# Cross-attention with layer norm: the last eight tiles in one written order, some residuals as identity products, and the last block's values' product in two halves

## The chip, the cores and the metric

The kernel runs on one core of one Trainium2 chip. Its time is the device time of one execution, in microseconds (us). A core has TensorE (PE, matrix products into PSUM), VectorE (DVE), ScalarE (ACT), GpSimd (POOL) and SyncE (SP), each with its own in-order instruction stream; they meet through semaphores. Loads, stores and copies are DMAs. SP, ACT and POOL each issue them in their own order, and all run on the same 16 DMA engines. Each text below that gives a time in us without more gives it from the start of the profiled span.

## The reference

Queries `x` (4 x 2048 x 512) attend to 77 context rows per batch, with 16 heads of 32; then a projection, a residual and a layer norm. All is float32.

```python
qs = (q @ wq).reshape(Bq, Lq, H, HD).transpose(0, 2, 1, 3)
ks_ = (k @ wk).reshape(Bq, Lk, H, HD).transpose(0, 2, 1, 3)
vs = (v @ wv).reshape(Bq, Lk, H, HD).transpose(0, 2, 1, 3)
scores = jnp.einsum('bhqd,bhkd->bhqk', qs, ks_) / jnp.sqrt(jnp.float32(HD))
scores = jnp.where(mask[:, None, :, :], -jnp.inf, scores)
attn_w = jax.nn.softmax(scores, axis=-1)
attn = jnp.einsum('bhqk,bhkd->bhqd', attn_w, vs)
...
out = attn @ wo + q
mu = jnp.mean(out, axis=-1, keepdims=True)
var = jnp.mean((out - mu) ** 2, axis=-1, keepdims=True)
return (out - mu) / jnp.sqrt(var + EPS) * gamma + beta
```

Here `k` and `v` are both the context, and the mask is the same for all rows of a batch.

## The kernel before, in words

The 8192 rows are cut into 64 tiles of 128 rows; two tiles make a block (32 blocks, 0 to 31), four tiles a group of the query projection. Keys and values of all batches are made once at the start. A tile then goes through these steps; names are those of the code.

1. `q_visit`, `q_evac` (L134, L145): a quarter of a group's queries on TensorE (12 products, each factor split into a high and a low float32r part), copied out by VectorE. They run five tiles ahead, so the last is issued in the slot of tile 58.
2. `scores` (L245): 16 products, one per head, into four PSUM banks. `maxima` (L262): VectorE adds the mask, writes the negated scores and keeps their minimum, one instruction per head. `exps` (L279): ACT's exponential, one per head, with the sum.
3. `recip` (L291) on VectorE and `normalise` (L295) on POOL divide by the sums; the last tile does it in two halves (`recip_half`, `normalise_half`).
4. `transp` (L314): VectorE transposes 32 x 32 squares of a tile into its half of the block's buffer `B`. `regroup` (L323): twelve SBUF-to-SBUF DMAs of 128 KB bring the squares of a block to the partitions of their keys, in `PT`.
5. `av` (L335): 16 products per block give the attention output, transposed. `av_hi` (ACT) and `av_lo` (VectorE) split it into two float32r parts, `AH` and `AL`.
6. `o_proj` (L370): 12 products per tile. `residual` (L385): VectorE adds the rows of `x`, loaded by `load_x` into one of eight buffers `o`. `moments` (L388): VectorE's statistics and aggregate, then POOL's power of -0.5, for two tiles at once.
7. `scale` (L412) on ACT and `affine` (L422) on POOL normalise; `store` (L427) on SP. For the last eight tiles `scale` is instead two VectorE instructions (subtract the mean and times gamma, times the root and plus beta), and there is no `affine`.

The order is written out by hand (`tc.manual_schedule()`): the order of the calls is the order of each engine's stream. A loop over pairs of tiles (L507) runs to the first half of slot 60; in slot u it does the scores of tile u, the projection of tile u - 6 or u - 5, and so on. L611 to L708 write out the rest. There block 30's twelve DMAs go to SP, SP and POOL in turn and block 31's to SP, ACT and POOL in turn; all others are SP's. One SP stream carries the x loads, the DMAs of `regroup` and the stores in the order of the calls; an x load must also wait until the tile eight before it is stored, since it takes its buffer. PSUM has eight banks, handed out in turn.

Of the kernel before, what the change touches and what calls it, by code (L numbers as in the profile page):

```python
# [36 lines left out]
TAILV = 8  # L37
LONE = 4
# [4 lines left out]
def xattn_layernorm(  # L43
# [39 lines left out]
    small = const.tile([P, 128], F32, name="small")  # L83
    mhalf, mneg, gates = small[:, 0:2], small[:, 2:4], small[:, 4:5]
# [218 lines left out]
    def recip_half(t, r):  # L303
        if r == 0:
            ris[t] = sb.tile([P, H], F32, tag="ri", bufs=3, name=f"ri_{t}")
        nc.vector.reciprocal(half_view(ris[t], r), half_view(sums[t], r))
# [7 lines left out]
    def transp(t):  # L314
        b, tt = divmod(t, 2)
        if tt == 0:
            bts[b] = sb.tile([P, 5, NP, 2, 32], F32, tag="B", name=f"B_{b}")
        nc.vector.transpose(  # L318
            bts[b][:, :, :, tt, :].rearrange("p c q r -> p q c r"),
# [3 lines left out]
    def regroup(b, queues=(nc.sync,)):  # L323
        pts[b] = sb.tile([P, 4, 2, NP * 2 * 32], F32, tag="PT", name=f"PT_{b}")
        pt = pts[b]
        bt = bts[b].rearrange("p c q t r -> p c (q t r)")
        n = 0
        for c in range(3):
            src = bt[:, 2:3].to_broadcast((P, 2, NP * 2 * 32)) if c == 2 else bt[:, c : c + 4 : 3]
            for i in range(4):  # L330
                queues[n % len(queues)].dma_start(pt[32 * c : 32 * c + 32, i], src[32 * i : 32 * i + 32])  # L331
                n += 1
# [17 lines left out]
    def av_hi(b, i):  # L350
        if i == 0:
            at[b] = [sb.tile([P, NG, BLK], F32R, tag=t, name=f"{t}_{b}") for t in ("AH", "AL")]
        nc.scalar.copy(at[b][0][:, 2 * i : 2 * i + 2], pas[b, i].rearrange("p (m r) -> p m r", m=2))

    def av_lo(b, i):
        hv = at[b][0][:, 2 * i : 2 * i + 2]
        pv = pas[b, i].rearrange("p (m r) -> p m r", m=2)
        nc.vector.tensor_tensor(at[b][1][:, 2 * i : 2 * i + 2], pv, hv.bitcast(F32), ALU.subtract)

    def av_evac(b):  # L360
        for i in range(2):
            av_hi(b, i)
            av_lo(b, i)
# [5 lines left out]

    def o_proj(t):  # L370
# [3 lines left out]
        pos[t] = bank(f"po_{t}")  # L374
        for c in range(NC_D):
            for n, (a, w) in enumerate(((ah, woh), (ah, wol), (al, woh))):
# [4 lines left out]
                    start=(c == 0 and n == 0),  # L381
# [6 lines left out]
    def moments(t):  # L388
# [9 lines left out]
        lone = t >= NT - LONE  # L398
        if lone or tt == 1:
            j = slice(tt, tt + 1) if lone else slice(0, 2)  # L400
            k = (t - tt) % TPB
            nc.gpsimd.tensor_tensor(rn[:, 0, j], mv[:, j, 1], nz[:, k + j.start : k + j.stop], ALU.add)
            nc.gpsimd.tensor_tensor(rn[:, 0, j], rn[:, 0, j], mhalf[:, j], ALU.pow)
            if t < NT - TAILV:
                nc.gpsimd.tensor_tensor(rn[:, 1, :], mv[:, :, 0], rn[:, 0, :], ALU.mult)
                nc.gpsimd.tensor_tensor(rn[:, 1, :], rn[:, 1, :], mneg, ALU.mult)

    def stats(t):
        residual(t)
        moments(t)  # L410

    def scale(t):  # L412
        o = od[t]
        b, tt = divmod(t, 2)
        mv, rn = mvs[b], rns[b]
        if t >= NT - TAILV:
            nc.vector.scalar_tensor_tensor(o, o, mv[:, tt, 0:1], gam, ALU.subtract, ALU.mult)  # L417
            nc.vector.scalar_tensor_tensor(o, o, rn[:, 0, tt : tt + 1], bet, ALU.mult, ALU.add)
        else:
            nc.scalar.activation(o, o, AF.Identity, bias=rn[:, 1, tt : tt + 1], scale=rn[:, 0, tt : tt + 1])  # L420
# [9 lines left out]

    nc.gpsimd.memset(mhalf, -0.5)
# [3 lines left out]
    warm = const.tile([P, D], BF16, name="warm")  # L435
    nc.vector.memset(warm, 0.0)
# [70 lines left out]
    for u in range(0, NT - 3, 2):  # L507
# [248 lines left out]
```

## Time and profile before

| what | value |
|---|---|
| runs shown | 547.81, 549.62, 550.54 us; median 549.62 |
| profiled execution, its own time | 546.65 us |
| its span | 544.7 us, mean granted TensorE clock 0.983 |
| busy share of the span | PE 96%, DVE 89%, ACT 85%, POOL 75% |
| scores of tile 56 start | 450.93 us |
| last projection (tile 63) ends | 530.5 us |
| last VectorE instruction ends | 541.55 us |
| store, from issue to landing, last stretch | 2.2 us (median) |
| x load, from issue to landing, last stretch | 3.6 us (median) |

In the lines of the trace, "line engine op, out<-in" names an instruction by its source line and the tiles it writes and reads; `po` is the projection's bank, `pa` the values' product, `sc` the scores, `nm` the row minimum. Busy times of PE come from a model of the pipelined ends of matmuls, so a busy PE is not one at its peak; what one matmul costs is read from one start to the next. SPq, DVEq and the like are an engine's sequencer, where a DMA issue or a wait stands. A wait is put down to the release that came last. The chain is the work that ended last, followed back from the end.

### The profile page before, as it was taken

How to read it: one execution, taken by the hardware profiler on the slowest of the kernel's cores; microseconds unless marked ns; L12 is line 12 of the kernel's file. 1: busy time of each engine (PE TensorE's matmuls, PEld its weight loads, DVE VectorE, ACT ScalarE, POOL GpSimd, SP SyncE). 2: the span in 40 equal slices, each digit the busy share in tenths (PEclk: the TensorE clock that was granted, in tenths of full speed). 3: DMA queues.
4: the chain of work that ended last, by engine and by line, in shares of the span. 5: the costliest groups of instructions: out<-in, count | busy, mean ns of one | idle time of the engine just before them, and what ended most of it. 6: DMA issues, size and time to landing. Idle time of an engine off the chain costs nothing.

```text
span 544.7 us, 15953 instructions
## 1 busy us (share of the span) xinstructions
PE 520.6 (96%) x4762; PEld 398.9 (73%) x4762; DVE 482.4 (89%) x2584; ACT 465.3 (85%) x2223; POOL 408.3 (75%) x354
## 2 busy tenths in 40 slices
PE   9999899999999999999999999999999999997790
PEld 6977577777777777777777777777777777775570
DVE  5687999989998889989998889989998889988677
ACT  5687799998899999998899999998899998889400
POOL 0526447888798988888798988888798986678651
PEclk9999999999999999999999999999999999998895
DMA  8935577778777877778778777778777766666752
GB/s 279 400 126 122 160 196 196 212 219 222 183 182 215 232 209 208 208 220 213 183 212 214 209 212 208 207 219 227 177 213 202 218 169 170 171 182 179 196 191 116
DMA packets 58982, 109.95 MB, mean 202 GB/s; under 512 B 9232, under 2 KB 10768, under 8 KB 58896
## 3 DMA queue, kind: packets, MB, share of 16 engines
q1 hardware_dynamic: 57088, 105.26, 69.8%
q0 software_dynamic: 1488, 3.15, 1.9%
q8 instruction: 38, 0.62, 0.5%
q10 hardware_dynamic: 320, 0.52, 0.3%
q14 instruction: 48, 0.39, 0.3%
HBM read 41.79 MB, written 16.78 MB: 108 GB/s over the span
## 4 chain that ended last, share of the span: by engine, by line
PE 79%; DVE 11%; SPq 4%; DMA 3%; issue 2%; ACT 1%; POOL 0%; DVEq 0%
PE po L377 29%; PE pq L131 27%; PE sc L254 11%; PE pa L342 10%; SPq L331 3%; DVE pbuf L268 3%; DVE B L318 2%; PE pk L157 1%; DMA stage_a<-wk 1%; DVE o L417 1%; DVE st L391 1%; DMA PT<-B 1%; DVE q L148 1%; DVE o L386 1%; ACT pbuf L282 1%
## 5 line engine op out<-in xcount | busy, mean ns | idle before, releaser
L282 ACT ACTIVATE pbuf<-pbuf,nm 128x77 f32<-128x77 f32 x1024 | 352.7, 352 | 34.6 <-DVE nm L268 33.1
L282 ACT ACTIVATION_READ_ACCUMULATOR pbuf<-pbuf,nm 128x1 f32 x1024 | 196.7, 192 | 0.0
L298 POOL TENSOR_TENSOR pbuf<-pbuf,ri 128x1232 f32<-128x1232 f32 x63 | 142.2, 2257 | 54.5 <-DVE ri L293 31.3
L268 DVE CUSTOM_DVE_ANT_0 pbuf<-sc,mb 128x77 f32<-128x77 f32 x1024 | 168.7, 231 | 5.4 <-PE sc L254 3.3
L377 PE MATMUL po<-woh,AH 128*128 128x512 f32 x256 | 107.4, 419 | 0.0
L318 DVE STREAM_TRANSPOSE B<-pbuf 128x1280 f32<-128x1280 f32 x64 | 95.6, 1493 | 7.4 <-DMA PT<-B 3.4
L377 PE MATMUL po<-wol,AH 128*128 128x512 f32 x256 | 101.1, 395 | 0.0
L377 PE MATMUL po<-woh,AL 128*128 128x512 f32 x256 | 100.6, 393 | 0.0
L131 PE MATMUL pq<-xth,wqh 128*128 128x512 f32 (+1 forms) x256 | 98.4, 384 | 1.3 <-DVE nm L268 1.3
L131 PE MATMUL pq<-xtl,wqh 128*128 128x512 f32 (+1 forms) x256 | 97.9, 382 | 0.0
L131 PE MATMUL pq<-xth,wql 128*128 128x512 f32 (+1 forms) x256 | 97.8, 382 | 0.0
L268 DVE DVE_READ_ACCUMULATOR2_ANT nm<- 128x1 f32 x1024 | 84.1, 82 | 0.0
L254 PEld LDWEIGHTS sc<-kct,q 32*128 32x128 f32 x2048 | 63.7, 186 | 22.5 <-issue 15.2
L425 POOL TENSOR_TENSOR o<-o,bet 128x512 f32<-128x512 f32 x56 | 73.3, 1310 | 4.4
L424 POOL TENSOR_TENSOR o<-o,gam 128x512 f32<-128x512 f32 x56 | 71.9, 1285 | 5.2 <-ACT o L420 5.2
L254 PE MATMUL sc<-kct,q 32*128 32x77 f32 x2048 | 73.4, 278 | 0.2 <-DVE nm L268 0.2
L342 PE MATMUL pa<-PT,vsb 96*32 96x256 f32 x1024 | 63.4, 388 | 6.9 <-DMA o<-x 3.8
L124 POOL TENSOR_TENSOR xtl<-xtf,xth 128x1024 fp32r<-128x1024 f32 x28 | 67.1, 2398 | 0.0
L377 PEld LDWEIGHTS po<-woh,AH 128*128 128x128 f32 x256 | 48.6, 190 | 24.3 <-DVE nm L268 9.0
L386 DVE TENSOR_TENSOR o<-po,o 128x512 f32<-128x512 f32 x64 | 43.9, 686 | 25.0 <-PE po L377 24.6
L131 PEld LDWEIGHTS pq<-xth,wqh 128*128 128x128 f32 x256 | 48.1, 188 | 11.8 <-DVE nm L268 2.3
L377 PEld LDWEIGHTS po<-woh,AL 128*128 128x128 f32 x256 | 48.5, 189 | 10.8
(87 smaller groups left out, 644.2 us busy)
## 6 DMA issues: line engine op xcount, KB each, us to landing
PT<-B SPq DMA_DIRECT2D x372, 128.0 KB, 2.4
o<-x SPq DMA_DIRECT2D x64, 256.0 KB, 5.2
out<-o SPq DMA_DIRECT2D x64, 256.0 KB, 2.7
xtf<-xT SPq DMA_DIRECT2D x28, 512.0 KB, 5.3
stage_a<-wq SPq DMA_DIRECT2D x4, 256.0 KB, 4.3
stage_a<-wk SPq DMA_DIRECT2D x4, 256.0 KB, 5.9
stage_b<-wv SPq DMA_DIRECT2D x4, 256.0 KB, 5.0
stage_a<-xT SPq DMA_DIRECT2D x2, 512.0 KB, 7.0
```

The source lines that it names most:

```text
L124: nc.gpsimd.tensor_tensor(l, fx.pop((g, c)), h.bitcast(F32), ALU.subtract)
L131: nc.tensor.matmul(pq, w[:, c, m * P : (m + 1) * P], r[:, c, rs], start=(n == 0), stop=(n == 11))
L254: nc.tensor.matmul(sc[j][:, g * NK : (g + 1) * NK], qs[q, g, rs], kct[q, g, t // TPB, keys_of(j)], start=True, stop=True,)
L268: nc.vector.tensor_tensor_reduce(pb[:, h // 2, (h % 2) * NK : (h % 2 + 1) * NK], scs[t][j][:, g * NK : (g + 1) * NK], mb[:, t % TPB, keys_ ...
L282: nc.scalar.activation(pb[:, h // 2, (h % 2) * NK : (h % 2 + 1) * NK], pb[:, h // 2, (h % 2) * NK : (h % 2 + 1) * NK], AF.Exp, bias=nmax[t ...
L298: nc.gpsimd.tensor_tensor(pv, pv, rv.to_broadcast((P, NP, 2, NK)), ALU.mult)
L318: nc.vector.transpose(bts[b][:, :, :, tt, :].rearrange("p c q r -> p q c r"), pbuf[t % NPB].rearrange("p q (c r) -> p q c r", c=5),)
L342: nc.tensor.matmul(pas[b, g // 2][HD * j : HD * (j + 1), (g % 2) * BLK : (g % 2 + 1) * BLK], vsb[:, 2 * b // TPB, HD * h : HD * (h + 1)], ...
L377: nc.tensor.matmul(pos[t], a[:, c, rs], w[:, c, :], start=(c == 0 and n == 0), stop=(c == NC_D - 1 and n == 2),)
L386: nc.vector.tensor_tensor(od[t], pos.pop(t), od[t], ALU.add)
L424: nc.gpsimd.tensor_tensor(o, o, gam, ALU.mult)
L425: nc.gpsimd.tensor_tensor(o, o, bet, ALU.add)
```

## The change

From slot 56 on, the loop and the written-out end are replaced by a string of 325 words, each one call of a helper, run in that order; so the streams of all engines are set by one list. A word is a letter and a tile (or block) number counted from tile 48 (block 24); T and e take a quarter of the heads, P and U one DMA of `regroup` with the queue that issues it (s is SP, a is ACT, g is POOL). Besides the order:

- Tiles 54, 55, 56, 57, 58, 60, 62 and 63 get their residual from TensorE: `resid` multiplies a 128 x 128 identity by the rows of `x` into the bank of the projection, which then accumulates on it. Statistics and centring of these tiles read PSUM.
- Fourteen tiles (50 to 63) end with `centre` and `finish` on VectorE, where eight did, and each has its own root on POOL (`rsqrt_one`).
- Block 31 is kept tile by tile in `B` and `PT`; `regroup_tile` issues twelve DMAs of half size for each tile, `av_tile` multiplies one tile, and the split into high and low parts goes by tile.
- The DMAs of blocks 27 to 31 are spread over SP and POOL, with ten on ACT.
- The identity is made once by POOL in slot 0, in the bytes of the tile that warms TensorE up.

```diff
@@ -34,8 +34,28 @@
 EPS = 1.0e-5
 WARM = 10
 NPB = 3
-TAILV = 8
-LONE = 4
+LAST = 16
+
+
+
+
+
+ORDER = """
+S8 Q8 q7 x4 T8.3 T8.0 e8.3 T8.1 T8.2 S9 k1 q8 x5 e8.1 f1 t7 S10 e8.2 T9.2 P3.7s O2 T9.0 k0 P3.1g x6 T9.1 e8.0
+P3.8s P3.10g T9.3 f0 P3.6s T10.2 Q9 e9.2 P3.9s T10.3 w1 +2 x7 e9.1 r8 T10.0 n8 w0 s2 P3.4s V2 e9.3 P3.11s T10.1
+q9 P3.5s e10.1 P3.3g y2 P3.0s S11 t8 v2 x8 a2.0 Q10 a2.1 P3.2g e9.0 b2.0 T11.3 T11.1 e11.3 r9 x9 T11.0 n9 O3
+b2.1 e10.0 q10 T11.2 e10.3 t9 S12 e10.2 z2 P4.5g P4.10s V3 T12.2 P4.4g w2 e11.1 r10 P4.8s P4.0g +3 n10 P4.2s
+T12.1 O5 e11.0 P4.7s s3 P4.1s e11.2 T12.0 P4.6s P4.3g y3 P4.9s t10 v3 S13 e12.2 P4.11s O4 a3.1 r11 T12.3 n11
+a3.0 T13.0 e12.1 b3.0 b3.1 e12.0 T13.1 S14 t11 e12.3 X6 z3 P5.5g O6 e13.1 T13.2 P5.10g w3 P5.0s T14.2 P5.4g
+e13.0 T13.3 P5.9g P5.3s r12 P5.2s T14.1 n12 V4 e13.2 P5.7s +4 P5.6s T14.0 e13.3 P5.8s s6 P5.11g S15 P5.1s T14.3
+a4.0 x10 y6 X7 a4.1 r13 e14.3 t12 n13 O7 e14.2 b4.0 T15.0 v6 e14.1 s4 V5 T15.1 v4 e14.0 b4.1 t13 X10 a5.1 e15.1
+X8 r14 P6.7g P6.1s y4 P6.9g X9 x11 T15.2 e15.0 P6.11s P6.4g z4 O8 P6.8g b5.1 w4 a5.0 P6.6g z6 e15.2 +5 n14 w6
+P6.2s T15.3 P6.10a O9 P6.3s h15.0 s5 P6.5a x12 m15.0 b5.0 P6.0s e15.3 s7 v5 t14 O10 y5 U14.9a U14.5g h15.1
+U14.10g y7 U14.3a U14.8g V6 z5 U14.0g U14.4a s8 w5 m15.1 U14.7s U14.6a s9 U14.11s X12 v8 t15 a6.0 O11 a6.1 v7
+x13 b6.0 U15.2a U15.7s b6.1 U15.4g U15.6s U14.2a y8 U15.5g U15.11s O12 z7 U15.0g U14.1a U15.8s y9 U15.10a x14
++11 v9 w7 s10 U15.1s U15.3g O13 z8 U15.9g y10 s11 v10 x15 s12 v11 W14 +13 v12 s13 W15 c14 y12 X14 c15 d14 v13
+d15 X15 z9 O14 y13 y11 z12 z10 w12 w8 O15 z11 z13 s14 w13 w11 y14 w10 w9 v14 s15 y15 v15 z14 z15 w14 w15
+"""
 KSCALE = 1.0 / HD**0.5
...
+    ident = const.tile([P, D // 2], F32, name="ident")
+    warm = ident.bitcast(BF16)
+    ident = ident[:, :P]
...
@@ -314,22 +337,32 @@
     def transp(t):
         b, tt = divmod(t, 2)
         if tt == 0:
-            bts[b] = sb.tile([P, 5, NP, 2, 32], F32, tag="B", name=f"B_{b}")
+            bts[b] = sb.tile([P, 5, 2 * NP * 32], F32, tag="B", name=f"B_{b}")
+        if b < NBLK - 1:
+            bt = bts[b].rearrange("p c (q t r) -> p c q t r", q=NP, t=2)[:, :, :, tt, :]
+        else:
+            bt = bts[b].rearrange("p c (t q r) -> p c q t r", q=NP, t=2)[:, :, :, tt, :]
         nc.vector.transpose(
-            bts[b][:, :, :, tt, :].rearrange("p c q r -> p q c r"),
+            bt.rearrange("p c q r -> p q c r"),
             pbuf[t % NPB].rearrange("p q (c r) -> p q c r", c=5),
         )
 
-    def regroup(b, queues=(nc.sync,)):
-        pts[b] = sb.tile([P, 4, 2, NP * 2 * 32], F32, tag="PT", name=f"PT_{b}")
-        pt = pts[b]
-        bt = bts[b].rearrange("p c q t r -> p c (q t r)")
-        n = 0
-        for c in range(3):
-            src = bt[:, 2:3].to_broadcast((P, 2, NP * 2 * 32)) if c == 2 else bt[:, c : c + 4 : 3]
-            for i in range(4):
-                queues[n % len(queues)].dma_start(pt[32 * c : 32 * c + 32, i], src[32 * i : 32 * i + 32])
-                n += 1
+    def regroup_part(b, n, queue, cols=slice(0, 2 * NP * 32)):
+
+        if b not in pts:
+            pts[b] = sb.tile([P, 4, 2, 2 * NP * 32], F32, tag="PT", name=f"PT_{b}")
+        c, i = divmod(n, 4)
+        bt = bts[b][32 * i : 32 * i + 32, :, cols]
+        src = bt[:, 2:3].to_broadcast((32, 2, cols.stop - cols.start)) if c == 2 else bt[:, c : c + 4 : 3]
+        queue.dma_start(pts[b][32 * c : 32 * c + 32, i, :, cols], src)
+
+    def regroup(b):
+        for n in range(12):
+            regroup_part(b, n, nc.sync)
+
+    def regroup_tile(t, n, queue):
+        tt = t % 2
+        regroup_part(t // 2, n, queue, slice(tt * NP * 32, (tt + 1) * NP * 32))
...
+    def av_tile(t):
+        b, tt = divmod(t, 2)
+        pt = pts[b].rearrange("p i a (t q r) -> p i a t q r", q=NP, t=2)
+        pas[b, tt] = bank(f"pa_{b}_{tt}")
+        for g in range(NG):
+            for j in range(GH):
+                h = g * GH + j
+                nc.tensor.matmul(
+                    pas[b, tt][HD * j : HD * (j + 1), g * P : (g + 1) * P],
+                    vsb[:, t // TPB, HD * h : HD * (h + 1)],
+                    pt[:NK2, :, h % 2, tt, h // 2],
+                    start=True,
+                    stop=True,
+                )
+
+    def at_part(b, k, i, by_tile):
+        if by_tile:
+            return at[b][k][:, :, i * P : (i + 1) * P], pas[b, i].rearrange("p (m r) -> p m r", m=NG)
+        return at[b][k][:, 2 * i : 2 * i + 2], pas[b, i].rearrange("p (m r) -> p m r", m=2)
...
+    def resid(t):
+        pos[t] = bank(f"po_{t}")
+        nc.tensor.matmul(pos[t], ident, od[t], start=True, stop=False)
 
     def o_proj(t):
         b, tt = divmod(t, 2)
         rs = slice(tt * P, tt * P + P)
         ah, al = at[b]
-        pos[t] = bank(f"po_{t}")
+        first = t not in pos
+        if first:
+            pos[t] = bank(f"po_{t}")
...
-                    start=(c == 0 and n == 0),
+                    start=(first and c == 0 and n == 0),
...
+    def moments_one(t):
+        st = sb.tile([P, 6], F32, tag="st", bufs=3, name=f"st_{t}")
+        nc.vector.bn_stats(st, pos.get(t, od[t]))
+        mvs[t, 1] = sb.tile([P, 4], F32, tag="mvt", bufs=LAST - 2, name=f"mvt_{t}")
+        nc.vector.bn_aggr(mvs[t, 1][:, :2], st)
+
+    def rsqrt_one(t):
+        mv = mvs[t, 1]
+        k = t % TPB
+        nc.gpsimd.tensor_tensor(mv[:, 2:3], mv[:, 1:2], bat[t // TPB][1][:, k : k + 1], ALU.add)
+        nc.gpsimd.tensor_tensor(mv[:, 2:3], mv[:, 2:3], mhalf[:, :1], ALU.pow)
+
+    def centre(t):
+        nc.vector.scalar_tensor_tensor(od[t], pos.pop(t, od[t]), mvs[t, 1][:, 0:1], gam, ALU.subtract, ALU.mult)
+
+    def finish(t):
+        nc.vector.scalar_tensor_tensor(od[t], od[t], mvs[t, 1][:, 2:3], bet, ALU.mult, ALU.add)
...
-    for u in range(0, NT - 3, 2):
+    for u in range(0, NT - LAST // 2, 2):
...
+            nc.gpsimd.memset(ident, 0.0)
+            nc.gpsimd.affine_select(ident, ident, [[-1, P]], ALU.not_equal, 1.0, base=0, channel_multiplier=1)
...
-    A, L = NT - 3, NBLK - 1
-    scores(A)
-    maxima(A, 0, H)
-    recip(A - 1)
-    normalise(A - 1)
-    affine(A - 8)
-    av(L - 3)
-    av_hi(L - 3, 0)
...
+    T0, B0 = NT - LAST, NBLK - LAST // 2
+    q4, by = H // 4, {"s": nc.sync, "a": nc.scalar, "g": nc.gpsimd}
+    one = {
+        "S": scores, "r": recip, "n": normalise, "t": transp, "W": av_tile, "x": load_x, "X": resid, "O": o_proj,
+        "+": residual, "s": moments_one, "v": rsqrt_one, "y": centre, "z": finish, "k": scale, "f": affine, "w": store,
+    }
+    for word in ORDER.split():
+        op, arg = word[0], word[1:]
+        k = None
+        if "." in arg:
+            arg, k = arg.split(".")
+        t, b = T0 + int(arg), B0 + int(arg)
+        if op in one:
+            one[op](t)
+        elif op in "Te":
+            (maxima if op == "T" else exps)(t, q4 * int(k), q4 * int(k) + q4)
+        elif op in "hm":
+            (recip_half if op == "h" else normalise_half)(t, int(k))
+        elif op in "Qq":
+            (q_visit if op == "Q" else q_evac)(*divmod(t + 5, 4))
+        elif op == "P":
+            regroup_part(b, int(k[:-1]), by[k[-1]])
+        elif op == "U":
+            regroup_tile(t, int(k[:-1]), by[k[-1]])
+        elif op == "V":
+            av(b)
+        elif op in "ab":
+            (av_hi if op == "a" else av_lo)(b, int(k))
+        else:
+            (av_hi if op == "c" else av_lo)(t // 2, t % 2, True)
```

## The prediction

> **What bounds the kernel now.** I read the page's slices first, to see which stages have slack. For 38 of 40 slices TensorE is full, so nothing outside it can matter there; the end is different.
>
> ```profile
> PE   9999899999999999999999999999999999997790
> DVE  5687999989998889989998889989998889988677
> ACT  5687799998899999998899999998899998889400
> POOL 0526447888798988888798988888798986678651
> ```
>
> Next the windows by stage, from the slot of tile 56 (its scores start at 450.93, by the timeline) to the end. Columns: window, its length, busy time of PE, weight loads, DVE, ACT and POOL, granted clock, DMA share, GB/s.
>
> ```profile
> 420.00:430.00 10.00, 10.00 (x123) 7.37 (x121) 9.77 (x65) 9.59 (x46) 8.45 (x9) 1.00 0.74 221
> 450.00:460.00 10.00, 10.00 (x117) 7.70 (x119) 9.77 (x57) 8.16 (x42) 6.59 (x8) 1.00 0.53 157
> 480.00:490.00 10.00, 9.81 (x98) 7.06 (x100) 9.90 (x68) 8.43 (x43) 6.82 (x8) 1.00 0.68 189
> 490.00:500.00 10.00, 7.23 (x99) 5.47 (x102) 8.50 (x47) 10.00 (x57) 8.30 (x7) 0.93 0.76 196
> 505.00:510.00 5.00, 2.00 (x9) 1.31 (x7) 2.93 (x6) 4.50 (x21) 2.89 (x3) 1.00 0.90 247
> 510.00:515.00 5.00, 4.18 (x37) 2.68 (x38) 3.40 (x4) 1.17 (x2) 2.50 (x5) 0.72 0.37 97
> 530.00:535.00 5.00, 0.49 (x3) 0.06 (x1) 4.69 (x9) 0.00 (x0) 1.16 (x2) 0.77 0.31 119
> 535.00:540.00 5.00, 0.00 (x0) 0.00 (x0) 4.72 (x9) 0.00 (x0) 1.15 (x2) 0.50 0.36 140
> ```
>
> The reader is to see two things. TensorE starves at 495 and 506 (and its clock falls with it), and it is done at 530.5, while VectorE then works alone for 11 us on a backlog that it could not start earlier. The chain of what ended last names both places, and VectorE's waits from 452 on say what it stood for:
>
> ```profile
> 495.18 2.40 DMA PT<-B
> 497.78 2.93 PE pa L342 x32
> 506.87 3.86 DMA o<-x
> 540.80 0.75 DVE o L418
> ```
>
> ```profile
> DVE AL L358 <- ACT AH L353: 4.2, 3, 3.0
> DVE o L386 <- PE po L377: 3.5, 3, 1.5
> DVE B L318 <- POOL pbuf L312: 2.0, 1, 2.0
> DVE ri L293 <- ACT pbuf L282: 1.3, 1, 1.3
> DVE ri L306 <- ACT pbuf L282: 0.4, 1, 0.4
> ```
>
> That is 11.4 us of standing. (The x load named at 506.87 rides behind the last PT pieces; the product needs the pieces.) So from 450.93 on the question is how densely VectorE's list can be packed, and whether TensorE's list is then still shorter.
>
> **Part by part: VectorE's list.** Before the new slots it ends the loop as it does now (first row maximum at 452.07). Start-to-start prices from the timeline: a row maximum 0.158 (16 took 2.53); a q copy, a low part (L358) 0.60; a reciprocal 0.17; a transpose 1.42; a residual add 0.70; statistics with aggregate 0.83; centre and finish together 1.47 (532.43 to 533.87 is 1.44, 538.44 to 539.95 is 1.51). Today: 128 maxima 20.2, 4 copies 2.4, 9 reciprocals 1.5, 9 transposes 12.8, 12 low parts 7.2, 14 adds 9.8, 14 statistics 11.6, 8 pairs 11.8, together 77.3. From 452.07 to the end of the last finish, 541.55, are 89.5, so 12.2 are idle, which agrees with the 11.4 of listed waits.
>
> The change takes 8 adds off (X on tiles 54 to 58, 60, 62, 63: -5.6) and brings 6 more pairs (tiles 50 to 55 get their scale and affine on VectorE: +8.8). The list grows to 80.5. So the change costs VectorE 3.2 and can win only out of the idle 12.2.
>
> How much idle stays? The densest stretches above (9.77, 9.77, 9.90 of 10) have 1.0 to 2.3% idle; with the list now offering at every point a finish, a centre or a quarter of maxima that needs nothing new, I take 2.3% of 80.5, 1.9, and one wait of the size that a residual had at 517 (0.5): 2.4. Bounds: 0.8 (the best stretch) and today's 12.2. I take the low side because the places of today's idle are covered by name: the low part's 4.2 and the transposes' 2.0 were chains with nothing else queued on VectorE, and the order now puts finishes (z3, z4, z6), centres and statistics of older tiles behind each.
>
> From the last finish to the end of the span is 544.7 - 541.55 = 3.15. New is that eight stores (2.1 MB) wait for the last eight microseconds, seven of them behind store 60 on SP's in-order queue. At 313 GB/s (517 to 519) they need 6.7, against about 7 that VectorE takes from that store's release to the last: 0.3 more.
>
> Sum: 452.07 + 80.5 + 2.4 + 3.15 + 0.3 = 538.4, against 544.7: 6.3 less.
>
> **TensorE's list**, which must stay shorter. Prices: scores 1.06, a q group 2.81, a values' product 1.86, an output projection 2.82. 8 scores 8.5, 3 groups 8.4, 5 products 9.3, the last block's two half products 1.9 (half the columns each), 14 projections 39.5, and 8 identity products. No full-array fp32 matmul is in the trace. The values' product moves 16 times 256 columns in 1.86 on a quarter of the columns of the array: 0.45 ns a column if nothing overlaps (512 columns: 0.23), 1.82 if four share the array (0.93). The scores move 16 times 77 in 1.06, which with four sharing is 3.4 ns (1.76). I take 0.93, from the longer rows, which are nearest in length; 7.4 in all, between 1.8 and 14.1. Sum 75.0, so 525.9 without a wait; behind the last projection follow statistics 0.83, two POOL steps 1.29 (0.605 and 0.684), a finish 0.75, hand-overs 0.25 and the store 3.45: 6.6, together 532.5. It may wait 5.9 before it decides. [...]
>
> **What is not on the path.** ACT from 452.4: 128 exponentials at 0.343 are 43.9, 12 casts 6.2, 2 scales 1.5 (6 scales fewer, -4.5), ten new DMA issues at 1.02 (4 took 4.08) 10.2: 61.8 of 80; the U issues stand behind the last exponentials, and only the casts of blocks 30 and 31 queue behind them. POOL: normalising 8 times 2.26 and 2 times 1.22, affines only for tiles 48 and 49 (5.3; six fewer, -16), 14 root pairs at 1.29, 27 DMA issues at 0.55 where 8 were: 59. A normalise can stand behind a root or a few issues, 1 to 2 us late, covered by the two tiles between it and its product. SP: 35 pieces, 12 loads and 16 stores at 0.60, 38. The identity's memset and select fall in POOL's 7.6 idle before 34.37; between 0.3 and 1.3 by its rows, hidden; were they not, the first normalise would be that much late. The last block's pieces go from 12 to 24 of half size, but over three queues; block 31's twelve took 8.3 from transpose to product today.
>
> [...] Eight statistics and eight centres now read PSUM instead of SBUF. By the rows, the add from PSUM (674 ns) costs no more than the statistics from SBUF (694) or the centre (732), and the copy from PSUM 669: no surcharge. [...]
>
> **Rivals.**
> - *The waits stay (slower).* TensorE is in order, and X15 stands ahead of the last two projections. Its load needs the buffer of tile 55, whose store stands behind finish 55 and ahead of the load on SP: 2.2 (median store in the last stretch) plus 3.6 (load) = 5.8 from store to data, against one projection, two half products and X14, 5.6, on TensorE. X14 and X12 hang in the same way. Each miss empties VectorE as 506 does now (3.86). If idle stays at 12.2, the span is 548.2, 3.5 more. It breaks even at 8.7 idle: two such misses. Against it: the buffers are eight deep and the other loads lie far ahead.
> - *TensorE becomes the bound.* At 1.76 an identity product the list is 81.7, to 532.6; with 4 of the 7.1 us of waits it has today after 495 (2.77, 3.82, 0.52), and 6.6 behind, 543.2, 1.5 less: no change to speak of.
> - *Denser still.* Idle 0.8 and stores unhindered: 536.5, 8.2 less.
>
> **How the numbers follow.** The profiled execution took 546.65 around its span of 544.7, and lies 3.0 under the median of 549.62 (547.81 to 550.54); I take the difference from the median. Forecast, 549.6 - 6.3 = 543.3, own range 541.8 to 546.0: 0.58. Denser, 541.4: 0.14. TensorE bound, 548.1: 0.14. Waits stay, 553.1: 0.14, some of it within half a per cent. Half a per cent is 2.75, about what a measurement of this kernel can tell from no change. Faster 0.58 + 0.14 + a little of the middle: 0.74; same 0.13; slower 0.13. The range takes the first three with the scatter of the median, 1: 540.3 to 549.0.
>
> **What would show it.** VectorE's waits after 452 sum to 3, not 11; no window of 5 us after 490 with VectorE under 4.4 before the last; TensorE's granted clock stays at 1.00 from 490 to 525; the last projection ends between 527 and 532; identity products near 0.93 start to start; centres near 0.73. Wrong would be: a wait of TensorE for an x load in front of L419, identity products over 1.5, or VectorE standing over 8.

## The result, and the profile after

The changed kernel takes 541.26 us (median of four, 540.0 to 543.51) against 548.71 (547.7 to 550.54) for the kernel before, measured together: a ratio of 0.9865, 95% interval 0.9817 to 0.9914. The profiled execution took 540.23 us around a span of 538.5, where the one before took 546.65 around 544.7. So it is 6.4 us less in the profiled pair and 7.5 in the medians; forecast were 6.3 less, a span of 538.4 and a median of 543.3.

First the page's slices of the kernel after, busy tenths of each fortieth of the span:

```profile
PE   8999899999999999999999999999999999999795
DVE  5688899889999898889998998889999988999977
```

VectorE and TensorE now go down together, in the last slice. Then the windows by stage, with the columns as shown of before, and the sums over all windows from 450 on:

```profile
490.00:500.00 10.00, 10.00 (x105) 5.98 (x97) 9.97 (x45) 8.91 (x46) 5.63 (x9) 1.00 0.41 105
505.00:510.00 5.00, 3.63 (x16) 2.66 (x15) 4.91 (x8) 0.78 (x5) 2.89 (x6) 1.00 0.91 261
510.00:515.00 5.00, 3.56 (x38) 2.20 (x39) 3.33 (x5) 1.17 (x2) 4.48 (x11) 1.00 0.76 236
520.00:525.00 5.00, 5.00 (x77) 3.82 (x76) 3.85 (x10) 0.97 (x2) 2.08 (x7) 1.00 0.20 56
525.00:530.00 5.00, 5.00 (x21) 3.62 (x20) 5.00 (x8) 0.20 (x1) 0.21 (x1) 1.00 0.06 24
530.00:535.00 5.00, 1.93 (x9) 1.27 (x7) 4.86 (x10) 0.00 (x0) 1.48 (x4) 0.91 0.76 290
...
sum 95.00, PE 76.53 PEld 55.62 DVE 79.70 ACT 53.14 POOL 53.37; mean PE 5.47 PEld 3.97 DVE 5.69 ACT 3.80 POOL 3.81
```

The starved window of before at 505 to 510 (TensorE 2.00, VectorE 2.93) has VectorE at 4.91 now, and the granted clock holds at 1.00 to 530. What is left of the hole lies at 508.6 to 511.4, on TensorE. VectorE's waits from 452 on (total, times, longest):

```profile
DVE o L439 <- PE po L430: 1.5, 2, 1.0
DVE AL L410 <- ACT AH L406: 1.1, 1, 1.1
DVE B L345 <- POOL mvt L483: 0.8, 1, 0.8
DVE st L475 <- PE po L430: 0.7, 1, 0.7
DVE B L345 <- POOL pbuf L335: 0.4, 1, 0.4
DVE pbuf L291 <- PE sc L277: 0.3, 1, 0.3
```

They sum to 4.8, where before had 11.4. TensorE's waits over the same time, 5.4 in all:

```profile
PE pa L375 <- DMA PT<-B: 2.8, 1, 2.8
PE po L430 <- DVE nm L291: 1.5, 2, 1.0
PE po L419 <- DVE nm L291: 1.1, 1, 1.1
```

And the chain of what ended last, in order of time (start, length):

```profile
508.80 2.66 DMA PT<-B
511.45 1.92 PE pa L375 x32
513.38 1.05 PE po L419 x2
514.43 8.22 PE po L430 x36
...
526.82 1.32 DVE o L486 x2
528.14 2.65 DVE o L489 x4
530.79 0.62 DVE st L475
```

It goes from the pieces through TensorE to the projection of tile 61, and then along VectorE to the end. TensorE's last product starts at 531.54, VectorE's last statistics at 532.32, the last finish ends at 535.34. Before, TensorE was done at 530.5, and VectorE worked on for 11 us more. (The chain's first line starts at 508.80, at an issue of POOL that by the order is a piece of tile 62; the wait is for block 30, whose last piece is SP's of 506.24, shown below.)

### The profile page after: what moved, and what is told of

Its sections match the earlier page's. It is cut to its first block, busy times and chain, and to the rows that moved or that the text cites. A ratio compares the mean times of both kernels' runs of the same rounds, so it can differ in the third digit from the quotient of the medians.

```text
span 538.5 us, 16101 instructions
## 1 busy us (share of the span) xinstructions
PE 522.8 (97%) x4810; PEld 398.9 (74%) x4810; DVE 483.6 (90%) x2588; ACT 462.6 (86%) x2217; POOL 404.5 (75%) x367
## 4 chain that ended last, share of the span: by engine, by line
PE 76%; DVE 13%; DMA 4%; SPq 2%; ACT 2%; issue 1%; POOL 1%; DVEq 0%; ACTq 0%
PE po L430 29%; PE pq L154 26%; PE sc L277 10%; PE pa L375 9%; DVE pbuf L291 4%; DVE B L345 3%; DMA PT<-B 3%; SPq L357 1%; ACT pbuf L305 1%; PE pk L180 1%; DMA stage_a<-wk 1%; DVE o L486 1%; DVE q L171 1%; DVE AL L410 1%; DVE o L489 1%
## 5 line engine op out<-in xcount | busy, mean ns | idle before, releaser
L305 ACT ACTIVATION_READ_ACCUMULATOR pbuf<-pbuf,nm 128x1 f32 x1024 | 216.4, 211 | 0.0
L291 DVE DVE_READ_ACCUMULATOR2_ANT nm<- 128x1 f32 x1024 | 84.7, 83 | 0.0
L277 PE MATMUL sc<-kct,q 32*128 32x77 f32 x2048 | 72.1, 277 | 0.0
L467 POOL TENSOR_TENSOR o<-o,bet 128x512 f32<-128x512 f32 x50 | 65.7, 1314 | 3.9
L466 POOL TENSOR_TENSOR o<-o,gam 128x512 f32<-128x512 f32 x50 | 64.3, 1286 | 0.2
L375 PE MATMUL pa<-PT,vsb 96*32 96x256 f32 x992 | 60.2, 382 | 3.0 <-DMA PT<-B 2.8
L439 DVE TENSOR_TENSOR o<-po,o 128x512 f32<-128x512 f32 x56 | 38.5, 687 | 22.4 <-PE po L430 22.2
```

Source lines behind the costliest of these rows:

```text
L277: nc.tensor.matmul(sc[j][:, g * NK : (g + 1) * NK], qs[q, g, rs], kct[q, g, t // TPB, keys_of(j)], start=True, stop=True,)
L291: nc.vector.tensor_tensor_reduce(pb[:, h // 2, (h % 2) * NK : (h % 2 + 1) * NK], scs[t][j][:, g * NK : (g + 1) * NK], mb[:, t % TPB, keys_ ...
L305: nc.scalar.activation(pb[:, h // 2, (h % 2) * NK : (h % 2 + 1) * NK], pb[:, h // 2, (h % 2) * NK : (h % 2 + 1) * NK], AF.Exp, bias=nmax[t ...
L375: nc.tensor.matmul(pas[b, g // 2][HD * j : HD * (j + 1), (g % 2) * BLK : (g % 2 + 1) * BLK], vsb[:, 2 * b // TPB, HD * h : HD * (h + 1)], ...
L439: nc.vector.tensor_tensor(od[t], pos.pop(t), od[t], ALU.add)
L466: nc.gpsimd.tensor_tensor(o, o, gam, ALU.mult)
```

## The experiments

To compare runs, the "stretch" is the span less the start of tile 56's scores (450.77 to 452.46 in all kernels): 93.8 us before, 87.2 after. The table has the profiled executions. VectorE's busy time is the sum of the windows from 450 to 545; "lost" is the time that TensorE's work in that stretch lost to a granted clock under 1.00 (busy time times what is missing from 1.00, by windows of 1 us).

| run | us | stretch | VectorE busy | VectorE waits | PE waits | lost |
|---|---|---|---|---|---|---|
| before | 546.65 | 93.8 | 78.0 | 11.4 | 6.8 | 3.4 |
| after | 540.23 | 87.2 | 79.7 | 4.8 | 5.4 | 0.0 |
| after_again | 543.01 | 90.4 | 79.2 | 8.3 | 5.7 | 3.1 |
| e1_no_ident | 545.17 | 92.5 | 84.7 | 4.7 | 10.8 | 3.9 |
| e9_before_ident | 549.99 | 96.3 | 77.0 | 16.0 | 7.6 | 6.5 |
| e2_whole_block | 543.4 | 90.4 | 80.0 | 7.8 | 5.4 | 3.3 |
| e3_one_queue | 546.23 | 93.0 | 82.0 | 8.8 | 8.2 | 3.4 |
| e4_ident_twice | 543.56 | 90.9 | 79.6 | 8.3 | 2.6 | 0.0 |
| e5_stats_twice | 548.84 | 94.6 | 86.3 | 6.8 | 7.5 | 2.6 |
| e7_four_act_pool | 548.58 | 95.3 | 75.1 | 17.8 | 7.8 | 6.2 |
| e6_piece_first | 539.64 | 86.6 | 79.8 | 4.2 | 4.8 | 0.0 |
| e8_both | 540.19 | 86.5 | 78.9 | 5.5 | 4.2 | 0.0 |
| e10_warm_after | 542.5 | 89.7 | 79.4 | 7.6 | 4.2 | 1.7 |
| e11_warm_before | 547.36 | 94.2 | 78.3 | 12.0 | 5.9 | 0.0 |

In nearly every row the stretch is VectorE's busy time plus its waits plus 2 to 3.5 (before has 4.4, e11 3.9, e5 1.5). That is bookkeeping, since VectorE works to the end in every kernel; it does not say what sets the end. The runs say what each part of the change does to these two terms. Those called e1 to e5, e7, e9 and after_again are single executions, run beside one of the kernel before (548.02 us for e1 to e4, 552.95 for the others), and the executions of the kernel before lie between 546.65 and 552.95.

**The same kernel again.** No edit.

> The changed kernel once more, to see how far the stretch from tile 56's scores to the end (87.2 in its profile) scatters between executions: every theory expects 87.2 within 0.5.

It took 543.01, 2.8 more than the profiled execution above, with the same list and 3.5 more of waits on VectorE. The stretch is 90.4, and not within 0.5 of 87.2 as expected. That is as much as several edits below move, so a single execution is read with the table, not by its time alone. The difference has a place. In windows of 1 us, this run of the unchanged kernel shows TensorE at half clock right behind the wait for block 30's pieces:

```profile
509.00:510.00 1.00, 0.00 (x0) 0.00 (x0) 0.62 (x2) 0.00 (x0) 1.00 (x2) 1.00 0.97 291
510.00:511.00 1.00, 0.00 (x0) 0.00 (x0) 0.95 (x1) 0.00 (x0) 0.88 (x4) 0.81 0.94 258
511.00:512.00 1.00, 0.79 (x8) 0.45 (x12) 0.56 (x1) 0.00 (x0) 0.69 (x2) 0.50 0.84 274
517.00:518.00 1.00, 1.00 (x5) 0.75 (x4) 1.00 (x2) 0.00 (x0) 0.00 (x0) 0.77 0.43 109
518.00:519.00 1.00, 1.00 (x6) 0.82 (x5) 0.20 (x1) 0.00 (x0) 0.00 (x0) 1.00 0.83 145
```

The wait was 3.1 here and 2.8 above, where the clock stayed up. The values' product then took 3.6 instead of 1.9, and the last product of TensorE started at 534.35 instead of 531.54.

**No identity products.** All X words dropped, the add of VectorE put back in front of the statistics:

```diff
-X6 ... X7 ... X10 ... X8 ... X9 ... X12 ... X14 ... X15
+(none)
-s6    s7    s8    s9    s10    s12    s14    s15
+ +6 s6 +7 s7 +8 s8 +9 s9 +10 s10 +12 s12 +14 s14 +15 s15
```

> The changed kernel without identity products: the eight residuals go back to VectorE as adds, each ahead of its tile's statistics; the order is otherwise the same. All runs of this study are compared by the stretch from the first scores of tile 56 to the end of the span: 93.8 us before the change, 87.2 in the changed kernel. Theory (VectorE's list, packed densely, sets the end): its list grows by 8 x 0.70 = 5.6; it stood for 4.8, and part of that is taken in: 89 to 93. Rival (TensorE's list sets the end as much, its last projection ends 0.4 us before the last tile's statistics start): it gets 8 x 0.86 = 6.9 shorter, so the loss is under 2: at most 89. Rival (the gain is the identity products' alone): back to 93 or more.

545.17. The sums of the same windows for this kernel:

```profile
sum 95.00, PE 73.51 PEld 54.12 DVE 84.73 ACT 52.43 POOL 54.41; mean PE 5.25 PEld 3.87 DVE 6.05 ACT 3.74 POOL 3.89
```

VectorE has 5.0 more to do than in the first profile after (79.70) and waits as little (4.7); the stretch is 5.3 longer. Against after_again, which also had a halved clock, VectorE has 5.6 more and waits 3.6 less, and the stretch is 2.1 longer. TensorE gains nothing from the work it is spared: it reaches block 30's product earlier and stands 6.0 us there, then runs it at half clock:

```profile
511.72 3.64 PE L375 MATMUL pa<-PT,vsb 96*32 96x256 f32 x32 [6.05 <-DMA PT<-B]
```

So in these executions the identity products are worth 2 to 5 us, all of it on VectorE. The new order without them takes 6.7 of waits off VectorE, and gives the time back through the six more centre and finish pairs: its stretch is 1.3 shorter than the one before, less than executions of one kernel differ by.

**Identity products in the kernel before.** Its last three tiles get them, at the end of their projection; order unchanged.

```diff
+XT = (61, 62, 63)
...
+        if t in XT:
+            nc.tensor.matmul(pos[t], ident, od[t], start=False, stop=True)
...
     def residual(t):
+        if t in XT:
+            return
```

> The kernel before with one part of the change alone: the residuals of its last three tiles as identity products, put behind the projection's twelve (their rows of x land late). VectorE works alone at that end, so each add that leaves it should shorten the stretch of 93.8 by its 0.70: 91.7 to 92.5. Rival (the identity products, 0.86 each on TensorE and ahead of the statistics, or rows of x that land after the projection, eat it): 93.5 or more.

A miss in this execution: 96.3, where I had expected 91.7 to 92.5. VectorE has 1.0 less to do and waits 4.6 more (16.0). TensorE's last product ends at 537.9 instead of 530.5: the stretch began 1.0 later, 3.1 more were lost to a halved clock (6.5, before 3.4), TensorE waited 0.8 more, and the three identity products stand at the end of their projections. But the clock's part comes and goes between executions of one kernel, and the kernel before, run beside this one, took 552.95 us, 3.0 more than its 549.99. So it is not shown whether identity products by themselves would shorten the kernel before.

**The last block's product in one piece.** Block 31 handled like the others:

```diff
-        if b < NBLK - 1:
+        if True:
...
-U14.9a ... U15.2a U15.7s ... W14 ... W15 c14 ... c15 d14 ... d15
+          P7.2a  P7.7s  ...       V7 a7.0 ... a7.1 b7.0 ... b7.1
```

> The changed kernel with block 31's values' product in one piece again, after the pieces of tile 63, and its twelve full-size transfers where tile 63's half-size ones stood. Theory: in the changed kernel's trace the two half products ran one right after the other (64 records from 522.57 on), so starting the first earlier was not what it gave; 86.5 to 88.5. Rival (the halves are a part of the gain, since the transfers of tile 62 are out of the way early): 89 or more.

The stretch is 90.4, which by the numbers set beforehand would be the rival's; but 3.3 are lost to the clock, as in after_again (90.4, 3.1), which has the halves. Waits and lists agree within 0.8. No worth of the halves is shown; in the changed kernel both half products run back to back anyway, in one group of 64 at 522.57.

**All pieces on SP.** Every P and U word issued by SP:

```diff
-P3.1g ... P6.10a ... U14.5g ... U15.10a
+P3.1s ... P6.10s ... U14.5s ... U15.10s
```

> The changed kernel with every transfer of blocks 27 to 31 on SP's queue, none on POOL's or ACT's, at the same places of the order. Theory (the spreading is needed, since SP's 72 pieces, 12 loads and 16 stores at 0.6 come in bursts and stand behind each other): the products of blocks 30 and 31 start 2 to 6 later: 89 to 93. Rival (the transfers share the same 16 engines, the queue only issues): 87.2 within 0.7.

The stretch is 93.0, 2.6 more than after_again at a like loss to the clock (3.4). The second half product now waits 3.1 us for its pieces, and TensorE's last product starts at 538.00. So the spread over three queues carries up to 2.6, at the last block. Not all of it need be the queue: with no pieces to issue, POOL normalises at other times, and meets VectorE's finishes (start, length):

```profile
497.90 2.61 POOL L321 TENSOR_TENSOR pbuf<-pbuf,ri 128x1232 f32<-128x1232 f32 x1 [1.95 <-DVE ri L316]
498.94 2.11 DVE L489 SCALAR_TENSOR_TENSOR o<-o,mvt,bet 128x512 f32<-128x512 f32 x1
```

This finish and one at 508.84 take 2.11 and 1.31 us, where the median is 0.74, and each ends 0.54 behind POOL's instruction. That is 1.9 of VectorE's 82.0, and the transpose of tile 63 starts at 511.69, 1.6 later than in after_again. The two causes are not told apart.

At block 30 the spread carries nothing: its product starts at 511.37 here and at 511.44 in the first profile after. The median landing of a full piece from SP, from 460 to 515, is 2.4 us before the change and 2.7 with the one queue:

```profile
PT<-B SPq DMA_DIRECT2D x46, 128.0 KB, 2.4
PT<-B SPq DMA_DIRECT2D x46, 128.0 KB, 2.7
```

The profile after has

```profile
PT<-B SPq DMA_DIRECT2D x26, 128.0 KB, 4.6
PT<-B POOLq DMA_DIRECT2D x16, 128.0 KB, 4.9
...
PT<-B ACTq DMA_DIRECT2D x2, 128.0 KB, 7.0
```

(queue, count, size, median us from issue to landing). Issued earlier by three queues, the pieces take longer by as much.

**Identity products twice.** Each preceded by a copy of itself that it overwrites, so that only TensorE has more to do:

```diff
+        nc.tensor.matmul(pos[t], ident, od[t], start=True, stop=True)
         nc.tensor.matmul(pos[t], ident, od[t], start=True, stop=False)
```

> The changed kernel with each of the eight identity products done twice (the second overwrites the first): TensorE's list is 8 x 0.8 = 6.4 longer, VectorE's the same. Theory (VectorE's list sets the end; TensorE stood for 5.4): 1 to 3 more, 88 to 90. Rival (TensorE's list sets it as much): 4 to 6.4 more, 91 to 93.6.

```profile
sum 95.00, PE 83.00 PEld 58.15 DVE 79.57 ACT 52.53 POOL 53.00; mean PE 5.93 PEld 4.15 DVE 5.68 ACT 3.75 POOL 3.79
```

TensorE is busy 6.5 us longer than after (76.53), 0.81 for each product; from one start to the next a product takes 0.86 (499.87, 500.73, 501.59, 502.45). The wait of 2.8 in front of block 30's product has gone, which leaves 3.7; and the stretch is 3.7 longer, 90.9 against 87.2, with no clock lost in either. VectorE's list is the same and its waits are 3.5 longer. That lies between what the theory (88 to 90) and the rival (91 to 93.6) had. TensorE has no slack left behind that wait.

**Statistics twice.** Only VectorE has more to do:

```diff
-        nc.vector.bn_stats(st, pos.get(t, od[t]))
+        for _ in range(2 if t >= NT - 8 else 1):
+            nc.vector.bn_stats(st, pos.get(t, od[t]))
```

> The changed kernel with the statistics of tiles 56 to 63 done twice over: VectorE's list is 8 x 0.73 = 5.8 longer, TensorE's the same. Theory (VectorE's list sets the end): 4 to 5.8 more, 91 to 93. Rival (TensorE sets it): under 2 more, below 89.2.

Eight more statistics at 0.69 are 5.5. The stretch is 4.2 longer than after_again (2.6 and 3.1 lost), 7.4 longer than after; 94.6 is above the 91 to 93 expected, which were set from an execution with no clock lost. So VectorE has little slack either: 4.2 of 5.5 show. By these two runs both lists bear on the end.

**Four tiles back to ACT and POOL.** Tiles 50 to 53 end with ACT's scale (K) and POOL's two affine products (f) instead of centre and finish; B is the root with two more small POOL instructions for the scale:

```diff
-v2 y2 z2 ... v3 y3 z3 ... v4 y4 z4 ... v5 y5 z5
+B2 K2 f2 ... B3 K3 f3 ... B4 K4 f4 ... B5 K5 f5
...
+    def act_scale(t):
+        mv = mvs[t, 1]
+        nc.scalar.activation(od[t], pos.pop(t, od[t]), AF.Identity, bias=mv[:, 3:4], scale=mv[:, 2:3])
```

> The changed kernel with tiles 50 to 53 finished as before the change, by ACT's scale and POOL's two affine instructions, at the places where finish stood: VectorE's list is 4 x 1.33 = 5.3 shorter, POOL's 4 x 3.4 = 13.6 longer, ACT's 3.0. Theory (the exchange is worth its 5.3 of VectorE time because POOL stands in front of the softmax of the next tiles): POOL's 2.7 per tile delays a normalise each time, 88 to 95. Rival (VectorE's list alone sets the end): shorter, 82 to 86.

VectorE has 4.6 less to do and waits 13 more. Its waits in this kernel name POOL's normalising:

```profile
DVE B L345 <- POOL pbuf L321: 7.6, 2, 4.1
DVE B L345 <- POOL pbuf L335: 4.2, 1, 4.2
```

An affine (two of 1.28 on POOL), placed where it waits for ACT's scale, holds up the normalise behind it, and with that the transposes: POOL stood 3.35 us for the scale ahead of the affine at 474.44, and its next normalise started at 478.68. So the time that these pairs cost VectorE keeps POOL free for the normalising, in these places at least: later ones were tried only for two tiles, below. (Of the 8.1 that the stretch is longer than after, a part may be the clock: 6.2 are lost here.)

**One piece ahead of the load.** Block 30's last SP piece stood behind the load of tile 60, which waits for the store of tile 52. SP's stream in the changed kernel (start, length):

```profile
505.85 0.34 SPq L415 DMA_DIRECT2D o<-x  x1
506.24 0.59 SPq L357 DMA_DIRECT2D PT<-B  x1
```

The word is moved in front of the load:

```diff
-x12 m15.0 b5.0 P6.0s e15.3
+P6.0s x12 m15.0 b5.0 e15.3
```

> The changed kernel with one word moved: the last SP piece of block 30 goes ahead of the load of tile 60, which waits on SP for the store of tile 52 to free its buffer. Theory (that load holds the piece back; the piece was issued at 506.24 and block 30's product waited 2.8 us until 511.44): the product starts 1.5 to 2.8 earlier, and the stretch of 87.2 gets 0.5 to 2 shorter, since VectorE's list had slack of 4.8. Rival (the product waits for landings on the shared DMA engines, not for this issue): the product no earlier than 510.5, stretch unchanged within 0.5.

Median 541.41 of four (538.64 to 543.25), ratio to before 0.9851, interval 0.9794 to 0.9908: not told apart from the change itself. In the profiled execution block 30's product starts 0.6 earlier (510.88). The three SP pieces are issued in one go from 501.26 and have gone out by 505.8, yet the last of the block's pieces is there only at 510.8, with the DMA engines (the share ahead of the last column) 97 to 98% busy:

```profile
500.00:505.00 5.00, 5.00 (x23) 3.94 (x22) 4.28 (x17) 3.68 (x21) 4.91 (x6) 1.00 0.98 285
505.00:510.00 5.00, 3.71 (x17) 2.74 (x15) 4.85 (x8) 0.84 (x6) 2.88 (x6) 1.00 0.97 246
```

As the rival had it, the product came no earlier than 510.5: the load at the head of SP's queue costs 0.6, not the 2.8 that the wait is long.

**That, and two late tiles off VectorE.** As above, with tiles 56 and 57 finished by ACT and POOL, late enough not to stand in front of a normalise:

```diff
-v8 ... y8 ... z8 ... v9 ... y9 ... z9
+B8 ... U15.10a K8 ... v10 f8 ... B9 K9 ... v13 f9
```

> The same move, and tiles 56 and 57 finished by ACT and POOL, which stand idle from 516 on, in place of VectorE's centre and finish (2.7 us off its list behind the last projections). Theory (both lists set the end, so both must get shorter): 1.5 to 3 shorter than 87.2. Rival (TensorE alone sets the end after the move): no shorter than with the move alone.

Median 540.48 of four (539.57 to 541.12), ratio to before 0.9838, interval 0.9788 to 0.9889. It is the lowest median of all; whether it is faster than the change (0.9817 to 0.9914) the runs don't tell. The stretch is 0.1 shorter than with the move alone, where 1.5 to 3 less than 87.2 was expected: the rival's case. VectorE has only 0.8 less to do than after, not 2.7, and waits 0.7 more. A part of what is missing is in two centres at 525.45, which take 2.6 us together instead of 1.3 while POOL's affine runs (525.91 to 527.54).

**Short products in the wait.** Is the halved clock behind the scatter, and can it be kept off? Ten 16-bit products on a constant go in front of block 30's product, into the bank that it overwrites:

```diff
             pas[b, i] = bank(f"pa_{b}_{i}")
+        for _ in range(10 if b == NBLK - 2 else 0):
+            nc.tensor.matmul(pas[b, 1], warm[:, :P], warm, start=True, stop=True)
```

> The changed kernel, with ten short 16-bit products on a constant (into the bank that the values' product then overwrites) in front of the values' product of block 30, so that TensorE works while it waits for the last PT piece. Ten such products should take about 2.2 us, within the wait of 2.8 to 3.1 us. Theory 1, the halved clock makes the scatter: of nine executions of the changed kernel and of the one with the piece ahead of the load, four had a mean granted clock of .996 or more and took 538.6 to 540.2 us, five had .991 to .993 and took 542.3 to 543.5; the two traces with .991 or so show half clock for 7 us right behind that wait, those with more show none. With the wait filled, every execution should be at .995 or more and between 538.5 and 541, median 540.0, against 541.26 for the change. Theory 2, the landing of the pieces makes the scatter and the clock only goes along: executions still spread from 539 to 543.5, median 541 to 542, with a clock of .993 or less in some.

Median 542.46 of six (539.85 to 543.07), ratio 0.9878, interval 0.9852 to 0.9904. As a remedy it failed: four of six still had a mean clock of .994 or .995 (542.4 to 543.1), two had .997 and .998 (539.85, 540.63). Time went with the clock again, but the filling didn't keep the clock up. In the profile the ten products take 2.3 us, the pieces land 0.7 later than in the first profile after, so 1.6 of idle stays, and the clock is halved a little behind it:

```profile
512.00:513.00 1.00, 0.88 (x17) 0.68 (x21) 0.00 (x0) 0.00 (x0) 0.83 (x2) 1.00 0.71 230
513.00:514.00 1.00, 1.00 (x20) 0.45 (x12) 0.08 (x1) 0.59 (x1) 0.98 (x3) 0.90 0.64 122
514.00:515.00 1.00, 1.00 (x5) 0.50 (x2) 0.79 (x2) 0.59 (x1) 0.92 (x3) 0.50 1.00 359
517.00:518.00 1.00, 1.00 (x6) 0.79 (x5) 0.49 (x1) 0.00 (x0) 0.00 (x0) 0.89 0.54 138
```

**The same in the kernel before.** Ten such products in front of the products of blocks 29 and 30, where before loses 3.4 to the clock:

```diff
+        for _ in range(10 if b in (NBLK - 3, NBLK - 2) else 0):
+            nc.tensor.matmul(pas[b, 1], warm[:, :P], warm, start=True, stop=True)
```

> The kernel before, with the same ten short products in front of the values' products of blocks 29 and 30, where it waits 2.8 and 3.8 us and then runs 3.9 and 3.5 us at half clock (3.4 us of TensorE's work lost together). If the clock was part of what the change won (TensorE's lateness is passed on to VectorE, which waits for projections and low parts in this stretch), the median falls by 2 to 3.4 to about 546.5 of 549.6, VectorE's waits after 452 fall from 11.4 to about 8 us, and the mean clock rises from .979 to .990. If the order on VectorE alone set the end, the time stays within 1 of 549.6 and VectorE's waits stay at 11, with the clock up all the same.

Median 548.35 of ten against 548.39 of sixteen, ratio 1.0, interval 0.998 to 1.002. The clock was higher (.980 to .989 against .977 to .982; no loss behind 450 in the profile), VectorE's waits stayed (12.0), and so did the median. But TensorE's last product started no earlier, at 530.90 against 530.10: the filling took the time that the clock gave. And within the ten, the six with a clock of .987 or more took 547.36 to 549.41 us, the four with .980 to .983 took 548.69 to 550.9. So a fuller clock bought with filling did not shorten the kernel before; whether the lost clock was on its path, and a part of what the change won, is not settled.

## Why the prediction was right, and where not

**The sum held, with two terms off against each other.** VectorE's list from tile 56's slot was put at 80.5, and measures 83.1 (452.22 to 535.34) less 4.8 of waits, 78.3. The mis-sized term is the price of a centre and finish pair, taken as 1.47 from starts to starts of before. In the profile after, such instructions stand back to back:

```profile
526.73 1.41 DVE L486 SCALAR_TENSOR_TENSOR o<-o,mvt,gam 128x512 f32<-128x512 f32 x2
528.06 2.73 DVE L489 SCALAR_TENSOR_TENSOR o<-o,mvt,bet 128x512 f32<-128x512 f32 x4
```

Two centres take 1.33 to the next start, and four finishes 2.65: 1.33 a pair. Fourteen pairs at 0.14 less are 2.0. The 1.44 and 1.51 of before were read where the two instructions of a tile follow each other; here they are grouped. That this is the 0.14 is the author's estimate from these starts; no run shows it alone. The other term is the idle time: 2.4 forecast, 4.8 measured. Together 82.9 forecast, 83.1 measured; that the two cancel is luck. The span of 538.5 is also that of an execution that lost nothing to the clock; after_again's is 541.2. The median of 541.26 lies 0.5 below the range of 541.8 to 546.0 given to this case and next to the 541.4 of "Denser still", whose condition, 0.8 of idle time, did not come: the list was shorter, not the idle time. The step that made the idle too small was to count only VectorE's own order and a wait of the size of a residual: 2.2 of the 4.8 are waits for a projection, and the projections are late by TensorE's 2.8 in front of block 30's product, which the prediction didn't foresee.

**TensorE's list was sized right, and its slack was spent.** 75.0 was forecast; from 451.28 to the end of the last projection at 531.9 are 80.6, less 5.4 of waits, 75.2. The identity product was put at 0.93 and measures 0.86 from one start to the next (experiment with two; three in a row after the change, 497.58 to 499.86 and some 0.3 until the projection's first start, give the same). "It may wait 5.9 before it decides": it waited 5.4, and decides as much as VectorE. So the rival "TensorE becomes the bound" had the wrong cause, the price of the product, but the right place: 0.5 us of slack, which any late landing or halved clock uses up. That fits the scatter of the changed kernel. Of the executions of it and of the one with the piece ahead of the load, those with a mean clock of .996 or more took 538.6 to 540.2, the others, at .991 to .993, 542.3 to 543.5.

**The rival "The waits stay" did not come, but its mechanism did, in another place.** The loads for tiles 62 and 63 were never waited for. The load of tile 60 stood at the head of SP's queue in front of a piece of block 30. Moving the piece brought 0.6, and the rest of that wait is the landing of the pieces themselves. They come slower than before: from 460 to 515 a full piece took a median of 4.6 us from SP, 4.9 from POOL and 7.0 from ACT, where before had 2.4, 3.5 and 5.1, and the one queue of the experiment 2.7; yet with the one queue block 30's product started no earlier. The DMA engines are 91 to 99% busy from 500 to 510 in the profile after, 81 to 83% with the one queue. The prediction counted the issuing time on each queue and took the landing as before; that step missed TensorE's 2.8. Its break-even of 8.7 idle was too low, by the 2.2 of the list and the 0.3 for the stores: after_again stood 8.3, and was still 3.5 shorter in span than the kernel before.

**By its own signs.** The last projection (531.9), the identity products, the centres and the clock to 525 came as listed in the first profile after. VectorE's waits were 4.8, not 3, and VectorE was under 4.4 in two windows before the last, 510 to 515 (3.33) and 520 to 525 (3.85). After_again, with its halved clock and 8.3 of standing, is past the mark of 8 that was to show the prediction wrong, and the kernel was faster even so. (Of the slices of before, 37 of 40 have TensorE at 8 tenths or more, not 38; nothing hangs on it.)

**Edits costed at nothing.** The identity's making (0.22 and 0.30 on POOL at 26.9) is hidden. The stores at the end cost nothing more: from the last finish to the end are 3.16, as the 3.15 of before, not 0.3 more. The half products are worth nothing that shows.

**Reading PSUM instead of SBUF.** Centres and statistics from PSUM and from SBUF, side by side in the profile after (minimum, median, maximum in ns):

```profile
L486 DVE SCALAR_TENSOR_TENSOR o<-po,mvt,gam x8: 701/745/751, 490.6 to 533.3; 128x512 f32<-128x512 f32 x8
L486 DVE SCALAR_TENSOR_TENSOR o<-o,mvt,gam x6: 657/745/748, 464.7 to 527.4; 128x512 f32<-128x512 f32 x6
L475 DVE BATCH_NORM_STATS2 st<-po x8: 666/690/700, 489.1 to 532.3; 128x6 f32<-128x512 f32 x8
L475 DVE BATCH_NORM_STATS2 st<-o x6: 645/689/695, 462.7 to 523.4; 128x6 f32<-128x512 f32 x6
```

The medians agree within 1 ns (745 and 745 for the centres, 690 and 689 for the statistics): the forecast was right to count nothing more for reading PSUM.

**What stays open.** Whether the halved clock is the cause of the 3 us by which executions of the changed kernel differ, or goes along with late pieces, is not settled: no run kept it off. For it speaks that 3.1 us of TensorE's work are lost in after_again, and the last projection is 2.8 later, with the wait only 0.3 longer. The 2 to 5 us for the identity products rest on single profiled executions, and what the order or the identity products would win alone is not shown.

## What to carry to other kernels

When one engine finishes a backlog alone at the end, write down its list and its standing time from the last full stage on: here the order took the standing (11.4 to 4.7 without identity products) while the identity products paid for most of the work that the order had added. Compare the slack of the next engine with the waits it already has before trusting the gain: here 5.9 of slack met 5.4 of waits, and what is left does not take in a late transfer. Before spreading a transfer over more queues, look at how busy the DMA engines are: here the issues came earlier, the engines were 91 to 99% busy from 500 to 510, and block 30's product came no earlier (511.44, and 511.37 with the one queue).

## What the runs showed that was not expected

- TensorE's granted clock, where it fell from 440 on ahead of TensorE's last product, stood at 0.50 for one of three lengths wherever the windows show the whole of it: 3.42 us in the windows of e10 (0.10, 0.50, 0.50, 0.50 and 0.11 short of 1.00, twice their sum of 1.71), in e3 at 512 and in both places of the kernel before (3.42 and 3.40); 6.82 to 6.84, twice that, in after_again, the whole-block run and e5 and in both places of e7 and of e9; and 10.24, three times the length, in the run without identity products. The length of the wait in front does not tell which: one of 2.82 kept the clock at 1.00 in the first profile after, one of 2.79 was followed by 6.84 at half clock in the whole-block run, and 1.56 behind the short products by 3.42.
- Which executions are hit differs from run to run of one kernel, and the mean clock of an execution goes with their number: in the profiles of the changed kernel, of e6, e8 and e10 it is .996 to .999 for none, .994 for one and .991 for two such lengths, at 539.6 to 540.2, 542.5 and 543.0 us.
- A 128 x 128 by 512 product of full float32 costs 0.86 us from one start to the next; the records say 592 ns, twice for each product.
- A finish on VectorE that starts while POOL normalises takes longer here: 2.11 and 1.31 us with one queue, 1.32 in the whole-block run, where 0.74 is the median, ending 0.54 or 0.55 behind POOL's instruction each time, as if it stood until then. The profile counts it as busy time, so no list of waits shows it; in the changed kernel's profile no finish met a normalising.
